# A recurrence of 64 blocks: which engine squares, sums and multiplies, and in which order the steps stand

## The chip, the cores and the metric

The kernel runs on one core of a Trainium2 chip. A core has five engines with instruction streams of their own: PE (TensorE, matrix products into PSUM), DVE (VectorE), ACT (ScalarE), POOL (GpSimd) and SP (SyncE, here only for starting transfers). They meet at semaphores. 16 DMA engines carry the transfers that SP and POOL start. The metric is the device time of one execution in microseconds; lower is better. Everything is float32.

## The reference, cut to what matters

The model has four layers on an image of 256 x 256 pixels with 128 channels, each of the form x + layer(group_norm(x)): an attention, a recurrence in the frequency domain, a triangle multiplication and a 3 x 3 convolution. The change lies in the second:

```python
forget_gate = sigmoid(x @ Wf + bf + 2.0)
input_gate  = sigmoid(x @ Wi + bi)
delta       = softplus(x @ Wd + bd) * 0.1
A_f, B_f    = fft2(padded A), fft2(padded B)      # complex, per channel
mag   = sqrt(Ar**2 + Ai**2 + 1e-08)
scale = 0.95 * sigmoid(mag) / (mag + 1e-08)
Ar, Ai = Ar * scale, Ai * scale
Bx_r, Bx_i = Br*x_r - Bi*x_i, Br*x_i + Bi*x_r
inp = delta * input_gate * Bx                     # both halves
# 16 times:
h_r, h_i = fg_r*(Ar*h_r - Ai*h_i) + inp_r, fg_i*(Ar*h_i + Ai*h_r) + inp_i
```

h starts at zero, and x + h goes to the third layer, whose group norm needs the mean and the mean square of x + h for every group of 4 channels.

## The kernel before

The 16 steps are not looped over. For each pixel and channel they are the power of a 2 x 2 matrix, and the kernel works out the power's coefficients from the trace t and the determinant d by repeated doubling (tr2, tr4, tr8 from tq2, tq4, tq8 and dn2, dn4, dn8), and then the sum of powers by one division, 1/(1 + d - t), made as an exponential of a logarithm.

The image is cut into NB = 64 blocks of 4 rows, 1024 pixels. The 128 channels are 64 real and 64 imaginary parts. In the recurrence's layout the 64 channels stand on half of the partitions, two of the block's rows on each half, so that a "wide" tile is 128 x 1024 (real and imaginary parts side by side) and a "thin" one is 128 x 512. A block goes through some 60 named steps. Those that the texts below speak of:

- ld: SP loads xf (channels by pixels, for the gates), xc (the same values in the layout of the recurrence) and hs (rows of the spectra of A and B).
- za, zb: the spectra of A and B in PSUM, from hs by PE. a2: the squares of A's parts (ACT; its tile is `a` in the profile). m2: their sum, |A|^2. lm, mg, lb, iv: the square root and the inverse of |A| by Ln and Exp on ACT; sg: the sigmoid; s: the scale. zaa: A copied to SBUF (`ar`).
- zd, zf, zi: the products of the gates; ab, ae, al_, q: softplus; f, ig: the sigmoids; fs_: f times s; ff: the product of f's halves, pf: their sum (POOL; tile `fs`). t (POOL) and d_ from these, D_ = d + 1 - t, lD and eD its inverse.
- p0, p1, bx: B times x. qg, v: the input term, in two halves.
- tq2 ... tq16, dn2 ... dn8 (squares on ACT), tr2 ... tr8, u2, u4, u8, xa, xb, be, e_, al: the doubling and the coefficients. xb is a sum on PE in PSUM (`pxb`).
- y0, y1, av, yf, yb and t1: A times v, times f, times its coefficient; and v times its own.
- ac1, ac2: the two terms are added to xc in SBUF by accumulating transfers that POOL starts. ev, bn: the sum and the sum of squares of the result, by ACT with an accumulator (tile `x2q`). st: the result goes to x2T in DRAM.

The steps are software-pipelined by hand. A list `order` holds pairs (step, lag); round `it` carries out each step for block it - lag, in the list's order, and `pin` holds each engine to that order. The loads are not pinned. So each engine's queue is fixed, and in it an instruction that waits holds up all behind it. The lags go to 4, so there are 68 rounds.

PSUM has three tags in this stage: "z" (two buffers of two banks, taken in turn by za, zb, zd, zf, zi), "y" (one buffer of two banks: av and bx) and "s" (two of one bank: m2 and pxb). `tt` and `stt` are two-input instructions on DVE (lines 995 and 1001 in the profile), `gt` one on POOL (998), `act` one on ACT (55), `mm` a matrix product (61). After the last round `warm` products keep PE running, the sums are reduced, and the triangle's stage begins with `tap_products` (products of the convolution's weights, for the fourth layer) and `group_affine` (the group norm's scale and shift from stats2).

Of the kernel before, what the change touches and what calls it, by code (L numbers as in the profile page):

```python
# [31 lines left out]
class Kernel:  # L32
# [50 lines left out]
    def group_affine(self, pool, psum, stats, tag, shift=None, mv=None, busy=8):  # L83
# [3 lines left out]
        pm = psum.tile([P, 2], F32, name=f"pm{tag}", tag="gn")  # L87
        d, v, mg, sd = (pool.tile([P, 1], F32, name=f"{n}{tag}") for n in ("gd", "gv", "mg", "sd"))
        if mv is None:
            mv = pool.tile([P, 2], F32, name=f"mv{tag}")  # L90
            V.tensor_reduce(mv, stats, AX.X, ALU.add)
            self.keep_busy(psum, busy)
            pin(self.mm(pm, self.g4n, mv))
            self.keep_busy(psum, 3)
            V.tensor_tensor(d, pm[:, 0:1], shift, ALU.add)
            V.scalar_tensor_tensor(v, d, d, pm[:, 1:2], ALU.mult, ALU.subtract)
            V.tensor_copy(mg, pm[:, 0:1])
            self.chain("table", self.act(sd, v, AF.Sqrt, bias=self.eps, scale=-1.0))
        else:
            self.keep_busy(psum, busy)  # L100
            pin(self.mm(pm[:, 0:1], self.g4, mv[:, 0:1]))
            self.keep_busy(psum, 3)
            V.tensor_copy(mg, pm[:, 0:1])
            V.tensor_sub(d, mv[:, 0:1], mg)
            V.scalar_tensor_tensor(v, d, d, mv[:, 1:2], ALU.mult, ALU.add)
            pv = psum.tile([P, 2], F32, name=f"pv{tag}", tag="gn")
            pin(self.mm(pv[:, 0:1], self.g4, v))
            self.keep_busy(psum, 3)
            self.chain("table", self.act(sd, pv[:, 0:1], AF.Sqrt, bias=self.eps))
# [797 lines left out]
    def recurrence(self, x1T, x2T, HD_, stats1, shift1, stats2, shift2):  # L907
# [7 lines left out]
        with ExitStack() as c:  # L915
# [39 lines left out]
            D = [{} for _ in range(NB)]  # L955
            parts = wp.tile([P, 2, 2, NB], F32, name="parts2")
            shiftc = wp.tile([P, 2], F32, name="shiftc")
            V.tensor_copy(shiftc, abc[:, :, 1])
            fold = wp.tile([P, HC], F32, name="fold")
            V.tensor_tensor(fold, self.ident[:, :HC], self.ident[:, HC:], ADD)  # L960
            rows = lambda t: t.rearrange("p i (r v) -> p r i v", v=N)
# [12 lines left out]
            def load(b):  # L974
                d = D[b]
                xf = d["xf"] = io.tile([P, 1024], F32, name="xf", bufs=2)
# [5 lines left out]
                d["hs"] = self.first_rows if b == 0 else self.row_transforms(io.tile([P, 2, HC], F32, name="hs", bufs=2), HD_, b)  # L982
# [34 lines left out]
            def total(d, name, pairs):  # L1017

                n = len(pairs)
                z = d[name] = ps.tile([P, n, 512], F32, name=name, tag="y" if n == 2 else "s", bufs=1 if n == 2 else 2)  # L1020
# [17 lines left out]
            def a2(d): act(rows(wide(d, "a2")), d["za"], AF.Square)  # L1038
            def m2(d): total(d, "m2", [[(self.ident, d["a2"][:, 0]), (self.ident, d["a2"][:, 1])]])
            def lm(d): act(thin(d, "mag"), d["m2"][:, 0], AF.Ln, bias=1e-8)  # L1040
# [5 lines left out]
            def ab(d): halves(d, wide(d, "az"), "d", "zd", AF.Identity)  # L1046
            def ae(d): act(wide(d, "ex"), d["az"], AF.Sigmoid, scale=-1.0)
            def al_(d): act(d["ex"], d["ex"], AF.Ln, bias=1e-37)
            def q(d): stt(wide(d, "q", 2), d["ex"], -1.0, d["az"], MUL, MAX)

            def sg(d): act(d["mag"], d["mag"], AF.Sigmoid)
            def s(d): tt(thin(d, "s", 3), d["mag"], d["inv"], MUL)
# [4 lines left out]
            def zaa(d): act(wide(d, "ar", 2), d["za"].rearrange("p r i v -> p i r v"), AF.Copy)  # L1057
# [3 lines left out]
            def t(d): gt(thin(d, "t", 3), d["fs"], d["ar"][:, 0], MUL)  # L1061
            def d_(d): tt(thin(d, "d"), d["m2"][:, 0], d["ff"], MUL)
            def D_(d): stt(thin(d, "D", 2), d["d"], 1.0, d["t"], ADD, SUB)

# [18 lines left out]
            def dn2(d): squared(d, "dn2", "d", 2)  # L1083
            def tr2(d): stt(thin(d, "tr2"), d["d"], -2.0, d["tq2"], MUL, ADD)
            def u2(d): gt(thin(d, "u2", 2), d["t"], d["tr2"], MUL)
            def tq4(d): squared(d, "tq4", "tr2")
# [3 lines left out]
            def tq8(d): squared(d, "tq8", "tr4")  # L1090
            def dn8(d): squared(d, "dn8", "dn4", 2)
# [3 lines left out]
            def xa(d): stt(thin(d, "g", 2), d["t"], -2.0, d["u8"], ADD, MUL)  # L1095
# [11 lines left out]
            def al(d): tt(d["t"], d["u8"], d["t"], SUB)  # L1107

            def y0(d): tt(wide(d, "y0"), d["ar"], both(d["v"][:, 0]), MUL)
            def y1(d): tt(wide(d, "y1"), d["ar"], both(d["v"][:, 1]), MUL)  # L1110
            def av(d): real_and_imaginary(d, "av", d["y0"], d["y1"])
            def yf(d): tt(wide(d, "yf", 2), d["av"], d["f"], MUL)
            def t1(d): (tt if last(d) else gt)(wide(d, "t1"), both(d["t"]), d["v"], MUL)
            def yb(d): tt(d["yf"], d["yf"], both(d["g"]), MUL)
# [13 lines left out]
            def ev_(d): statistic(d, 0, AF.Identity)  # L1128
            def bn(d): statistic(d, 1, AF.Square, shifted=True)
            def st(d):  # L1130
                b = d["b"]
                for half in range(2):
                    dst = x2T[:, b * 1024 + half * 512:b * 1024 + (half + 1) * 512]
                    pin(nc.gpsimd.dma_start(dst.rearrange("(r c) n -> c r n", c=HC), d["xc"][half * HC:(half + 1) * HC]))
            def ld(d): load(d["b"])
# [3 lines left out]
                (e_, 3), (ld, 0), (za, 0), (u4, 2), (zb, 1), (a2, 0), (av, 2), (t, 1), (p1, 1), (zaa, 0), (m2, 0),  # L1139
                (tq8, 2), (al, 3), (zd, 0), (ev_, 4), (lD, 2), (q, 1), (yf, 2), (p0, 1), (tq2, 1), (dn2, 1), (tr2, 1),  # L1140
                (eD, 2), (tr8, 2), (lm, 0), (dn8, 2), (mg, 0), (ab, 0), (t1, 3), (qg, 1), (lb, 0), (tq16, 2), (bx, 1),
                (ac1, 3), (iv, 0), (u8, 2), (yb, 3), (zf, 0), (sg, 0), (tq4, 1), (v, 1), (y1, 1), (f, 0), (xa, 2),
                (D_, 1), (s, 0), (u2, 1), (ac2, 3), (tr4, 1), (ae, 0), (fs_, 0), (zi, 0), (y0, 1), (ff, 0), (pf, 0),
                (xb, 2), (ig, 0), (be, 2), (al_, 0), (bn, 4), (d_, 0), (dn4, 1), (st, 4),
            )
            deep = max(lag for _, lag in order)
            for it in range(NB + deep):
                for step, lag in order:
# [3 lines left out]
            warm = ps.tile([P, 1, 512], F32, name="warm", tag="s")  # L1152
            for _ in range(56):
                pin(self.mm(warm[:, 0, :P], self.ident, self.cmat))
            red = wp.tile([P, 2, 2], F32, name="partsum")
            V.tensor_reduce(red, parts, AX.X, ADD)
            pr = ps.tile([P, 2], F32, name="partps", tag="s")
            for ri in range(2):
                self.mm(pr[ri * HC:(ri + 1) * HC], fold, red[:, :, ri])
            V.tensor_copy(stats2[:, :, 0], pr)  # L1160

    def triangle(self, x2T, x3T, znT, prodD, rs2D, rs3D, stats2, shift2, stats3, shift3, prepare):
# [12 lines left out]
        with ExitStack() as c:  # L1175
            wp = c.enter_context(self.pool(name="tw", bufs=1))
            with self.pool(name="twp", bufs=2, space=PSUM) as ps0:
                self.tap_products(ps0)
                ab, mg, _ = self.group_affine(wp, ps0, stats2, "2", shift=shift2, busy=0)
# [351 lines left out]
    def tap_products(self, ps):  # L1531

        W, V = self.weights, self.nc.vector
        kt, wd = W["kt"], W["wd"]
        pb = ps.tile([P, 2], F32, name="cpb", tag="gn")
        self.mm(pb[:, 0:1], wd, W["bv"])
        V.tensor_copy(W["bw"], pb[:, 0:1])
        for t in range(3):
            pk = ps.tile([P, 3, P], F32, name="cpk")
            for n in range(3):  # L1540
                self.mm(pk[:, n], kt[:, 3 * t + n, :], wd)
            V.tensor_copy(kt[:, 3 * t:3 * t + 3, :], pk)
# [178 lines left out]
    def run(self, ctx):  # L1721
# [10 lines left out]
        stats["2"] = const.tile([P, 2, 1], F32, name="stats2")  # L1732
        shift2 = const.tile([P, 1], F32, name="shift2")
# [87 lines left out]
```

## Time and profile before

| | |
|---|---|
| time, median of 3 runs | 4684.48 us (4682.95 to 4684.81) |
| profiled execution: its own time, its span | 4678.77 us, 4677.0 us |
| busy share of the span: PE, DVE, ACT, POOL | 97%, 80%, 71%, 45% |
| recurrence, first matmul of za to the first of the sums at the end | 1649.8 to 2973.6 us |
| DMA share and rate in the recurrence (1712 to 2894 us) | 0.57 of 16 engines, 131 GB/s |

The profile is of one execution, the trace behind it lists each instruction with its engine, start, duration and what released it. Three things help in reading it. A row of the groups gives busy time, mean duration and the idle time of the engine ahead of it; durations of neighbours on an engine overlap by some hundredths of a microsecond, so a sum of durations is a little over the time from start to start. An instruction that stands still after it has begun counts as busy: its duration grows, and no idle time shows. And the busy share of the whole span says little here, since the four layers have different limits; the windows give it by stage.

### The profile page before, as it was taken

What the parts mean: (1) busy time and instruction counts of PE and PEld (TensorE: products, weight loads), DVE (VectorE), ACT (ScalarE), POOL (GpSimd) and SP (SyncE); (2) the same over time, 40 slices, a digit from 0 to 9 for tenths busy, and PEclk for the clock granted to TensorE, in tenths of its full rate; (3) what the DMA queues carried; (4) which work ended last, traced back from release to release, by engine and by line L of the source; (5) the groups of instructions that cost most, each with busy time, mean ns of one, the idle gap of its engine ahead of it and who ended that gap; (6) DMA issues with size and microseconds to landing.
All of it is one profiled execution on the core that took longest, in us unless ns stands there. A gap on an engine that the chain in (4) does not pass through costs nothing. (4 is left out here: it accounts for less than half of the span.)

```text
span 4677.0 us, 79571 instructions
## 1 busy us (share of the span) xinstructions
PE 4521.0 (97%) x30445; PEld 2600.4 (56%) x30445; DVE 3750.3 (80%) x4827; ACT 3333.0 (71%) x5173; POOL 2101.5 (45%) x1379
## 2 busy tenths in 40 slices
PE   8999999999999989999999999899999999999999
PEld 2444555555555533333333333456999973379999
DVE  7776777777777679999999999787666677789885
ACT  7556888888888889999999999798443454442110
POOL 1333555555555547667666667333231245520000
PEclk9999999999999999999999999999999999999999
DMA  9892122222222235555555555576667758955432
GB/s 316 327 357 110 54 83 82 87 82 82 85 88 82 69 88 132 134 133 130 134 130 133 136 129 126 184 253 246 243 222 262 251 211 327 360 208 174 135 114 72
DMA packets 219655, 768.19 MB, mean 164 GB/s; under 512 B 58443, under 2 KB 60620, under 8 KB 178926
## 3 DMA queue, kind: packets, MB, share of 16 engines
q1 hardware_dynamic: 153976, 465.15, 29.2%
q0 software_dynamic: 65232, 297.90, 22.2%
q8 instruction: 244, 4.00, 0.3%
q14 instruction: 139, 1.14, 0.1%
q10 hardware_dynamic: 64, 0.00, 0.0%
HBM read 431.32 MB, written 265.55 MB: 149 GB/s over the span
## 5 line engine op out<-in xcount | busy, mean ns | idle before, releaser
L629 DVE TENSOR_TENSOR e<-sc,bT 128x1024 f32<-128x1024 f32 x512 | 613.8, 1220 | 255.8 <-PE sc L61 254.8
L629 POOL TENSOR_TENSOR ks<-e 128x1024 f32<-128x1024 f32 x256 | 602.4, 2371 | 443.2 <-PE nd L61 429.9
L55 ACT ACTIVATE e<-e 128x1024 f32<-128x1024 f32 x512 | 539.3, 1053 | 40.3 <-DVE e L629 30.7
L61 PE MATMUL m<-U,v 128*128 128x128 f32 x4608 | 514.8, 275 | 1.5 <-DVE v L1656 1.5
L61 PEld LDWEIGHTS m<-U,v 128*128 128x128 f32 x4608 | 514.6, 192 | 1.7 <-DVE v L1656 1.7
L61 PEld LDWEIGHTS z<-wf,zt 128*128 128x128 f32 x4096 | 462.6, 192 | 53.6 <-DVE LR L1169 28.0
L61 PE MATMUL z<-wf,zt 128*128 128x128 f32 x4096 | 474.8, 277 | 5.6 <-DVE LR L1169 5.5
L1169 DVE TENSOR_TENSOR LR<-z,sg 128x512 f32<-128x512 f32 (+1 forms) x323 | 270.0, 867 | 165.3 <-ACT sg L55 165.3
L1169 POOL TENSOR_TENSOR zt<-zt,df 128x512 f32<-128x512 f32 x127 | 161.5, 1271 | 423.2 <-ACT df L55 423.2
L55 ACT ACTIVATE sg<-z 128x512 f32<-128x512 f32 (+1 forms) x323 | 160.7, 509 | 243.7 <-PE z L61 241.4
L61 PE MATMUL sc<-proj 32*128 32x256 f32 x4096 | 300.5, 404 | 3.2 <-DVE e L629 2.4
L998 POOL TENSOR_TENSOR fs<-f 128x512 f32<-128x512 f32 x64 | 176.4, 2756 | 275.1 <-DVE f L995 251.1
L61 PEld LDWEIGHTS sc<-proj 32*128 32x128 f32 x4096 | 188.5, 185 | 161.8 <-PE px L61 94.8
L61 PE MATMUL nd<-e,proj 128*32 128x256 f32 x4096 | 273.7, 385 | 2.6 <-DVE og L629 2.6
L55 ACT ACTIVATE dn<-dn 128x512 f32<-128x512 f32 x384 | 237.9, 620 | 12.5 <-DVE dn L629 8.5
L1696 ACT COPY m4s<-m 128x512 f32<-128x512 f32 x32 | 18.7, 585 | 304.3 <-PE m L61 304.3
L61 PE MATMUL z<-LR 128*128 128x256 f32 x1024 | 225.5, 383 | 7.5 <-DVE LR L1169 7.5
L998 POOL TENSOR_TENSOR u<-t,tr 128x512 f32<-128x512 f32 x64 | 225.6, 3525 | 11.9 <-DVE tr L1001 10.1
L998 POOL TENSOR_TENSOR t<-t,v 128x1024 f32<-128x1024 f32 x63 | 206.9, 3285 | 50.2 <-DVE t L995 49.5
L1706 POOL DMA_DIRECT2D out_dram<-ys x32 | 37.0, 1157 | 420.9 <-DVE ys L1704 420.9
L61 PEld LDWEIGHTS z<-LR 128*128 128x128 f32 x1024 | 196.6, 192 | 35.5 <-DVE LR L1169 8.3
L1169 POOL TENSOR_TENSOR zt<-ga,zt 128x1024 f32<-128x1024 f32 x62 | 144.7, 2353 | 118.5 <-DVE ga L1169 118.5
(430 smaller groups left out, 10738.4 us busy)
## 6 DMA issues: line engine op xcount, KB each, us to landing
zt<-znT SPq DMA_DIRECT2D x96, 1024.0 KB
zt<-x2T SPq DMA_DIRECT2D x64, 1024.0 KB
xin<-in_x_dram SPq DMA_DIRECT2D x48, 1024.0 KB
xr<-x3T SPq DMA_DIRECT2D x46, 768.0 KB
x1T<-x POOLq DMA_DIRECT2D x64, 512.0 KB, 5.0
xf<-x1T SPq DMA_DIRECT2D x64, 512.0 KB
xc<-x1T SPq DMA_DIRECT2D x128, 256.0 KB
x2T<-xc POOLq DMA_DIRECT2D x128, 256.0 KB, 3.7
```

Source lines behind the costliest of these rows:

```text
L55: return self.nc.scalar.activation(out, in_, func, bias=bias, scale=scale, **kw)
L61: return self.nc.tensor.matmul(out, lhsT, rhs, start=start, stop=stop)
L629: pin = lambda f: lambda *a, **k: tc.keep_in_program_order(f(*a, **k))
L998: pin(nc.gpsimd.tensor_tensor(out, a, b_, op))
L1169: pin = lambda f: lambda *a, **k: tc.keep_in_program_order(f(*a, **k))
L1696: nc.scalar.copy(m4, m[4])
L1706: nc.gpsimd.dma_start(out[row:row + 8].rearrange("r p t c -> p (r t) c"), ys.rearrange("p g k t c -> p (g k t) c"))
```

## The change

What it does, by engine:

- |A|^2 (m2) is no longer two products on PE into PSUM: a2's first half gets its second added by an accumulating transfer that POOL starts (block 0: by DVE). lm and d_ read it from SBUF.
- The spectrum of A is made twice: za as before, and zc in the next round. ar holds only its real part, half the size, for t; y0 and y1 read zc in PSUM.
- The sum of the result (ev) is no longer taken by ACT: each block's xc is added to a tile `summed` by an accumulating transfer that POOL starts, reduced once at the end. The last block's sum is still ACT's.
- d_, al and yb go from DVE to POOL, u2 and t1 from POOL to DVE. st is started by SP, not by POOL.
- xf has one buffer, not two; hs four, not two; az, ex, a2, s, t, D, tq4, tq8 and others have other counts. Tag "s" in PSUM has one buffer; a bank is taken by `spare`, for `awake`.
- The order and the lags are new: the path to t and d is one round longer (lb, iv, sg, s, fs_, ff, pf, d_ at lag 1), the doubling of tr2 to u2 is at lag 2.
- tap_products comes ahead of the third round. The mean and mean square of the groups come from `folded` at the end of the recurrence, so that group_affine needs no reduction and no product for them.

```diff
-    def group_affine(self, pool, psum, stats, tag, shift=None, mv=None, busy=8):
+    def group_affine(self, pool, psum, stats, tag, shift=None, mv=None, busy=8, means=None):
...
+            if means is None:
+                ...
+            else:
+                pm = means
...
+            spare = ps.tile([P, 512], F32, name="spare", bufs=1)
+            def awake(n):
+                for _ in range(n):
+                    pin(self.mm(spare[:, :P], self.ident, self.cmat))
+            V.memset(parts, 0.0)
+            summed = io.tile([P, 2, 512], F32, name="summed", bufs=1)
+            nc.gpsimd.memset(summed, 0.0)
+            folded = wp.tile([P, HC], F32, name="folded")
+            V.tensor_tensor(folded, self.g4n[:, :HC], self.g4n[:, HC:], ADD)
...
-                xf = d["xf"] = io.tile([P, 1024], F32, name="xf", bufs=2)
+                xf = d["xf"] = io.tile([P, 1024], F32, name="xf", bufs=1)
...
-                ... self.row_transforms(io.tile([P, 2, HC], F32, name="hs", bufs=2), HD_, b)
+                ... self.row_transforms(io.tile([P, 2, HC], F32, name="hs", bufs=4), HD_, b)
...
-                z = d[name] = ps.tile([P, n, 512], F32, name=name, tag="y" if n == 2 else "s", bufs=1 if n == 2 else 2)
+                z = d[name] = ps.tile([P, n, 512], F32, name=name, tag="y" if n == 2 else "s", bufs=1)
...
-            def a2(d): act(rows(wide(d, "a2")), d["za"], AF.Square)
-            def m2(d): total(d, "m2", [[(self.ident, d["a2"][:, 0]), (self.ident, d["a2"][:, 1])]])
-            def lm(d): act(thin(d, "mag"), d["m2"][:, 0], AF.Ln, bias=1e-8)
+            def a2(d): act(rows(wide(d, "a2", 2)), d["za"], AF.Square)
+            def m2(d):
+                if d["b"]:
+                    pin(nc.gpsimd.dma_start(d["a2"][:, 0], d["a2"][:, 1], accum_op=ADD))
+                else:
+                    tt(d["a2"][:, 0], d["a2"][:, 0], d["a2"][:, 1], ADD)
+            def lm(d): act(thin(d, "mag"), d["a2"][:, 0], AF.Ln, bias=1e-8)
...
-            def zaa(d): act(wide(d, "ar", 2), d["za"].rearrange("p r i v -> p i r v"), AF.Copy)
+            def zaa(d): act(thin(d, "ar", 2).rearrange("p (r v) -> p r v", v=N), d["za"][:, :, 0], AF.Copy)
...
-            def d_(d): tt(thin(d, "d"), d["m2"][:, 0], d["ff"], MUL)
+            def d_(d): gt(thin(d, "d"), d["a2"][:, 0], d["ff"], MUL)
...
-            def u2(d): gt(thin(d, "u2", 2), d["t"], d["tr2"], MUL)
+            def u2(d): tt(thin(d, "u2", 2), d["t"], d["tr2"], MUL)
...
-            def al(d): tt(d["t"], d["u8"], d["t"], SUB)
-            def y0(d): tt(wide(d, "y0"), d["ar"], both(d["v"][:, 0]), MUL)
-            def y1(d): tt(wide(d, "y1"), d["ar"], both(d["v"][:, 1]), MUL)
+            def al(d): gt(d["t"], d["u8"], d["t"], SUB)
+            def zc(d): spectrum(d, 0, "zc")
+            def turned(d, n, k):
+                v = d["v"][:, k].rearrange("p (r v) -> p r v", v=N).unsqueeze(2).to_broadcast([P, 2, 2, N])
+                tt(rows(wide(d, n)), d["zc"], v, MUL)
+            def y0(d): turned(d, "y0", 0)
+            def y1(d): turned(d, "y1", 1)
...
-            def t1(d): (tt if last(d) else gt)(wide(d, "t1"), both(d["t"]), d["v"], MUL)
-            def yb(d): tt(d["yf"], d["yf"], both(d["g"]), MUL)
+            def t1(d): tt(wide(d, "t1"), both(d["t"]), d["v"], MUL)
+            def yb(d): gt(d["yf"], d["yf"], both(d["g"]), MUL)
...
-            def ev_(d): statistic(d, 0, AF.Identity)
+            def ev_(d):
+                if last(d):
+                    statistic(d, 0, AF.Identity)
+                else:
+                    pin(nc.gpsimd.dma_start(summed, d["xc"], accum_op=ADD))
...
-                    pin(nc.gpsimd.dma_start(dst..., d["xc"][half * HC:(half + 1) * HC]))
+                    pin(nc.sync.dma_start(dst..., d["xc"][half * HC:(half + 1) * HC]))
...
             order = (
-                (e_, 3), (ld, 0), (za, 0), (u4, 2), (zb, 1), (a2, 0), (av, 2), (t, 1), (p1, 1), (zaa, 0), (m2, 0),
-                (tq8, 2), (al, 3), (zd, 0), (ev_, 4), (lD, 2), (q, 1), (yf, 2), (p0, 1), (tq2, 1), (dn2, 1), (tr2, 1),
-                (eD, 2), (tr8, 2), (lm, 0), (dn8, 2), (mg, 0), (ab, 0), (t1, 3), (qg, 1), (lb, 0), (tq16, 2), (bx, 1),
-                (ac1, 3), (iv, 0), (u8, 2), (yb, 3), (zf, 0), (sg, 0), (tq4, 1), (v, 1), (y1, 1), (f, 0), (xa, 2),
-                (D_, 1), (s, 0), (u2, 1), (ac2, 3), (tr4, 1), (ae, 0), (fs_, 0), (zi, 0), (y0, 1), (ff, 0), (pf, 0),
-                (xb, 2), (ig, 0), (be, 2), (al_, 0), (bn, 4), (d_, 0), (dn4, 1), (st, 4),
+                (q, 1), (ld, 0), (zd, 0), (tq2, 2), (tr2, 2), (ab, 0), (tq4, 2), (za, 0), (dn2, 2), (D_, 2), (lD, 2),
+                (zb, 1), (a2, 0), (qg, 1), (lb, 1), (av, 2), (iv, 1), (ac2, 4), (tr4, 2), (tq8, 2), (e_, 3), (zaa, 0),
+                (u2, 2), (dn4, 2), (p0, 1), (dn8, 2), (p1, 1), (yb, 3), (zf, 0), (eD, 2), (yf, 2), (zi, 0), (tr8, 2),
+                (al, 3), (u4, 2), (m2, 0), (ev_, 4), (sg, 1), (st, 4), (ae, 0), (f, 0), (bx, 1), (t1, 3), (s, 1),
+                (ac1, 3), (ig, 0), (u8, 2), (fs_, 1), (tq16, 2), (xa, 2), (ff, 1), (pf, 1), (d_, 1), (t, 1), (al_, 0),
+                (zc, 1), (lm, 0), (xb, 2), (v, 1), (bn, 4), (y0, 1), (mg, 0), (y1, 1), (be, 2),
             )
             for it in range(NB + deep):
+                if it == 2:
+                    self.tap_products(ps)
...
-            warm = ps.tile([P, 1, 512], F32, name="warm", tag="s")
-            for _ in range(56):
-                pin(self.mm(warm[:, 0, :P], self.ident, self.cmat))
+            awake(56)
+            V.tensor_reduce(parts[:, 0, :, 0:1], summed, AX.X, ADD)
...
+            for n, m in enumerate((folded, fold)):
+                for ri in range(2):
+                    pin(self.mm(pr[ri * HC:(ri + 1) * HC, n], m, red[:, :, ri]))
+            awake(3)
...
-                self.tap_products(ps0)
-                ab, mg, _ = self.group_affine(wp, ps0, stats2, "2", shift=shift2, busy=0)
+                ab, mg, _ = self.group_affine(wp, ps0, stats2, "2", shift=shift2, means=self.means2)
```

In tap_products itself the products and copies are pinned, and its tiles take tag "s".

## The prediction

> **What bounds the kernel now.** I read the windows by stage first. The changed stage, the recurrence, runs from about 1650 to 2974 us. Its steady part was cut at the start of one DVE instruction (`q<-q,ig`, step qg) in two blocks 51 apart, 1832.29 and 2860.40:
>
> ```profile
> core 0: us, PE busy (x) PEld busy (x) DVE busy (x) ACT busy (x) POOL busy (x), PEclk, DMA share, GB/s
> 1712.00:2894.00 1182.00, 1121.29 (x3410) 393.36 (x3409) 1173.96 (x1470) 1173.95 (x1986) 808.96 (x469) 1.00 0.57 131
> 1832.29:2860.40 1028.11, 976.19 (x2959) 341.85 (x2958) 1020.40 (x1277) 1022.50 (x1735) 698.79 (x409) 1.00 0.57 132
> ```
>
> 1028.11/51 is a period of 20.16 us a block. ACT is busy 20.05 of it, DVE 20.01, PE 19.14, POOL 13.7; TensorE's granted clock is 1.00, so there is no throttle to win back. Two engines are full. Which one binds is told by the DVE's and POOL's timelines (start, duration), two excerpts of each:
>
> ```profile
> 1891.54 0.69 DVE L1001 SCALAR_TENSOR_TENSOR tr<-d,tq 128x512 f32<-128x512 f32 x1 [0.34 <-ACT tq L55]
> 1892.15 0.68 DVE L1001 SCALAR_TENSOR_TENSOR tr<-dn,tq 128x512 f32<-128x512 f32 x1
> 1892.75 2.30 DVE L995 TENSOR_TENSOR q<-q,ig 128x1024 f32<-128x1024 f32 x1
> ...
> 2215.88 1.22 DVE L995 TENSOR_TENSOR q<-q,ig 128x1024 f32<-128x1024 f32 x1
> ...
> 2218.75 1.21 DVE L1001 SCALAR_TENSOR_TENSOR v<-q,bx 128x1024 f32<-128x1024 f32 x1
> ```
>
> ```profile
> 1892.33 1.65 POOL L998 TENSOR_TENSOR u<-t,tr 128x512 f32<-128x512 f32 x1
> ...
> 2215.49 4.48 POOL L998 TENSOR_TENSOR u<-t,tr 128x512 f32<-128x512 f32 x1
> ```
>
> In two blocks of three POOL's u stands still under DVE instructions with two SBUF inputs (qg, u4, yb) and ends when v, with one input in PSUM, has run: 4.48 us for 1.3 us of work. In the third block DVE has caught up with ACT and waits 0.34 us for tq; POOL gets in, and qg stands still: 2.30 for 1.22. The 2.30 rows stand 60.47 us apart, three blocks. Between them DVE's block is 19.65 (tr4 at 1852.42 and 1872.08). So ACT binds at 20.05 to 20.16; DVE alone would need 19.65.
>
> The rows that the change touches (1700 to 2900, 60 blocks; busy, mean ns, idle), DVE, ACT, PE, POOL:
>
> ```profile
> L995 DVE TENSOR_TENSOR y<-ar,v 128x1024 f32<-128x1024 f32 x119 | 145.4, 1221 | 2.0
> L995 DVE TENSOR_TENSOR u<-u,tr 128x512 f32<-128x512 f32 x119 | 81.3, 683 | 0.0
> L995 DVE TENSOR_TENSOR yf<-yf,g 128x1024 f32<-128x1024 f32 x59 | 71.7, 1216 | 0.0
> L995 DVE TENSOR_TENSOR d<-m,ff 128x512 f32<-128x512 f32 x60 | 40.8, 680 | 0.0
> ```
>
> ```profile
> L55 ACT ACTIVATE x2q<-xc 128x512 f32<-128x512 f32 x118 | 74.0, 627 | 1.9
> L55 ACT ACTIVATE ar<-za 128x1024 f32<-128x1024 f32 x60 | 60.8, 1013 | 0.0
> ```
>
> ```profile
> L61 PE MATMUL m<-a,ident 128*128 128x512 f32 x240 | 118.6, 617 | 24.1 <-ACT a L55 24.1
> L61 PE MATMUL za<-ev,hs 14*128 14x512 f32 x240 | 67.6, 640 | 0.0
> ```
>
> ```profile
> L998 POOL TENSOR_TENSOR t<-t,v 128x1024 f32<-128x1024 f32 x60 | 198.0, 3300 | 42.4 <-DVE t L995 41.7 <-DMA hs<-HD 0.7
> L998 POOL TENSOR_TENSOR fs<-f 128x512 f32<-128x512 f32 x60 | 167.0, 2783 | 233.9 <-DVE f L995 233.9
> ```
>
> **The change, per block.** *ACT.* ev goes (two x2q with their accumulator reads: 2211.55 to 2212.92, 1.37), ar is halved (0.91 from start to start becomes about 0.48, a 512 row's), lm reads SBUF (+0.04): 20.05 - 1.37 - 0.43 + 0.04 = 18.3. Table loads stay two a block, since Ln/Exp and Sigmoid steps are still in two groups.
>
> *DVE.* From start to start a 512 instruction costs 0.60, a 1024 one 1.14 (2215.88 to 2217.01). Off: d_ and al (0.60 each) and yb (1.14). On: u2 (0.60), t1 (1.14). That is -0.60. y0 and y1 now read zc in PSUM in a strided order; nearest are yf<-av,f (PSUM, plain, 1217 ns, as dear as SBUF) and p (PSUM, strided, 740 against 684 for 512): between 0 and +0.11 each; I take +0.06 each. 19.65 - 0.60 + 0.12 = 19.17.
>
> *PE.* m2 goes (118.6/60 = 1.98), zc comes (za's row, 1.13): 19.14 becomes 18.3. In the new order zb waits for ab to free zd's buffer, about 0.45. By distances of starts (zf 1.77, bx 3.6, pxb 2.6, za 0.95) the round is 18.0, with that wait 18.4.
>
> *POOL.* u2 and t1 leave; d_, al and yb come; st's two issues (1.30) move to SP, and m2 and ev are two issues more (0.9 each, by xc<-t's 0.94). Unblocked work: 512 1.30 (t<-fs,ar), 1024 2.36 (t<-t,v in the tail). When can it run? The Trainium skill (SBUF — State Buffer, Who interferes with whom) has VectorE with two SBUF inputs and GpSimd reading SBUF exclude each other for a whole instruction. The excerpts agree, which speaks against more POOL work: 5 x 1.3-2.4 = 7.6 us has to lie where DVE reads PSUM or rests. By the rule alone those 7.6 us and DVE's 11.2 us of two-SBUF work (four of 1.14, eleven of 0.60) fill 18.8 of a round of 19.17, and nothing is lost; by the trace an instruction that enters at the wrong time costs the other engine 1.08 (2.30 - 1.22), five of them 5.4. Which it is, the order decides. So I lay DVE out by starts: q 0, tr2 1.13, D_ 1.73, qg 2.33, tr4 3.46, e_ 4.06, u2 4.66 (all SBUF); p0 5.26, p1 6.57, yf 7.88 (PSUM); tr8 9.02, u4, t1 10.22, s, u8, fs_ 12.56, xa 13.70, ff 14.30 (SBUF); v 14.90, y0, y1, be (PSUM), end about 19.17. yb and al need 3.66 in the first gap of 3.76; pf, d_ and t, whose input ff ends at 14.98, need 3.9 in the second of 4.2. Both fit, barely. I add 0.1 for overlaps at their ends: **19.27 a block**.
>
> *What the new waits hold up.* t (POOL) ends about 18.9 and releases tq2, then tr2, due at 1.13 of the next round: about 0.5 spare. Behind it ACT has ab, tq4, dn2 for tr4 at 3.46, 0.4 spare, if zd ends by 0.7. u2 on DVE needs only t and tr2, which are there. POOL's queue: ac2 waits for ac1's landing (issued 11.5, 4.9 to land, needed at 19), ev for ac2's (landed about 6, needed 10), then ac1; ev may be 3 us late before pf is. m2 is issued at about 9 and lm, its reader, comes at 16.4, against 4.9 for twice the bytes. DMA: queue 0 took 38.4% of 1200 us, 7.7 a block for 1.5 MB; 0.75 MB more, 3.9, brings the share from 11.5 of 20.16 to some 15.4 of 19.27. SP: xf 0.34, xc 1.35, eight hs 7, st 1.30, 10 of 19; st waits for ac2, with the next loads behind it, at a time when these need xf's buffer anyway. xf has one buffer now: its load starts after zi (about 10.5) and zd wants it at 18.
>
> *Ends.* tap_products moves from PE's path before pm (2973.9 to 2978.4) into the third round: three turns of 1.45 matmul, 0.56 copy and handovers, 6.6, partly beside a pipe still filling (DVE busy 41.3 of the first 62): +4. In the triangle's start gd comes 4.8 earlier (2979.03 against about 2974.2), but the loads of zt still go out at 2974: -3.5. ev of the block before the last leaves ACT's tail: -1.5. For the last block yb and al on POOL in line (3.66) replace 2.6 on the DVE: +1. Sum 0; from -6 to +7.
>
> **Sum.** 64 x (20.16 - 19.27) = 57. The profiled execution (span 4677.0, 4678.8 in all) would become 4621.8; the median of the runs lies 5.7 above it, so 4684.5 - 57 = **4627.5**.
>
> **Rivals.** *Single xf buffer (PE late).* Two transfers of 512 KB took 2201.5 to 2206.2 together, 0.21 MB/us. Beside m2, ev and ac1 xf gets half: 4.7 us plus issue and landing, at 16 to 17, 1 to 2 before zd's need. If it takes over 7.5 us, zd, ab, dn2 and tr4 slip. Half a microsecond late: 19.75, 4684.5 - 26 = 4658. For: SP's queue is in order, with hs between. Against: the room.
> *POOL takes the port (slower).* yb is queued from about 0.8 while DVE runs q to u2. If DVE pauses there (tq2 over 0.5 late, or dn2), yb starts and holds the port 2.36; the next DVE instruction waits about 2.15 (1.08 per 1.30 in the trace, less the overlap). In every block: 21.4, +80, 4764. It eats the gain from 0.89/2.15 = 41% of the blocks. For: the trace shows just this for u, one block in three. Against: there ACT was the late one; it has 0.9 spare now, and fs, queued behind f in the same way, lost 60 of 60 times (2778 to 2796 ns).
> *The transfers do not do what they should.* An accumulation within SBUF of 256 KB is not in the trace. From 3.0 to 7.2 us (the extremes of xc's transfers, issue to landing) it is hidden; at 9.2 us lm waits 1.9, ACT is at 20.2 again, and the time stays 4684. For: two transfers more on one queue. Against: its half size, and that nothing else of that queue is under way at 9.
>
> **How the numbers follow.** Laid out as above 0.62 (19.1 to 19.55: 4610 to 4650); xf late 0.16 (faster); port taken 0.16, of which slower 0.12 and within the bound 0.04; transfers 0.06, of which faster 0.01, same 0.03, slower 0.02. Faster by over 0.2% (9 us, what a measurement here can tell): 0.79; same 0.07; slower 0.14. The range 4606 to 4684 leaves out the slower cases and the edges.
>
> **What would show it.** Right: 19.2 to 19.4 a block; DVE 99%, ACT about 95%; rows x2q<-xc only at the end; yb starting as p0 does, about 2.4 long after its wait; ff at 684 ns. Wrong: DVE rows of 2.3 to 3.5 us among D_, qg and ff; lm waiting for a DMA; zd waiting for xf; PE's clock below 1.00 in the middle.

## The result, and the profile after

The change makes the kernel slower: 4782.5 us (median of 4 runs, 4779.5 to 4786.8) against 4684.65 for the kernel before (4 runs, 4682.95 to 4684.9). The ratio is 1.0214, 95% interval 1.0202 to 1.0226. The forecast was 4627.5. What came is the rival "POOL takes the port", in every block, and a second loss that had no price in the forecast: TensorE's clock.

The windows of the changed kernel, from one start of qg to the start 50 blocks later (the columns are those of the windows of before):

```profile
1796.84:2877.58 1080.74, 1012.66 (x2900) 344.34 (x2899) 1061.44 (x1202) 938.43 (x1501) 639.04 (x450) 0.93 0.75 160
```

1080.74/50 is 21.615 us a block; before it was 20.16. DVE is busy 98% of it, ACT 87%, PE 94%, and TensorE's granted clock has fallen from 1.00 to 0.93. So ACT was relieved as planned, and DVE has become the full engine, at a block 2.3 us longer than the 19.27 worked out for it. Where those are is read from DVE's timeline, with POOL's beside it:

```profile
2202.50 1.22 DVE L1015 SCALAR_TENSOR_TENSOR q<-ex,az 128x1024 f32<-128x1024 f32 x1
2203.64 2.83 DVE L1015 SCALAR_TENSOR_TENSOR tr<-d,tq 128x512 f32<-128x512 f32 x1
...
2218.98 0.68 DVE L1009 TENSOR_TENSOR ff<-f 128x512 f32<-128x512 f32 x1
2220.34 1.22 DVE L1015 SCALAR_TENSOR_TENSOR v<-q,bx 128x1024 f32<-128x1024 f32 x1 [0.68 <-PE bx L61]
2221.66 2.35 DVE L1009 TENSOR_TENSOR y<-zc,v 128x1024 f32<-128x1024 f32 x2
2224.17 0.69 DVE L1015 SCALAR_TENSOR_TENSOR g<-pxb,D 128x512 f32<-128x512 f32 x1 [0.15 <-PE pxb L61]
```

```profile
2202.67 3.25 POOL L1012 TENSOR_TENSOR yf<-yf,g 128x1024 f32<-128x1024 f32 x1
```

yb is issued 0.17 us after q has begun, stands until q is through, and then runs for its 2.36 us. tr2, which reads two tiles in SBUF, stands for that time: 2.83 us for 0.68. (This exclusion of DVE and POOL is what the texts call the port.) As with qg before, the time shows as a long instruction and not as idle time. It is so in every block, as the groups tell (busy and mean duration, then the idle time ahead):

```profile
L1015 DVE SCALAR_TENSOR_TENSOR tr<-d,tq 128x512 f32<-128x512 f32 x51 | 145.0, 2843 | 0.0
L1009 DVE TENSOR_TENSOR y<-zc,v 128x1024 f32<-128x1024 f32 x102 | 120.1, 1219 | 5.3
L1009 DVE TENSOR_TENSOR ff<-f 128x512 f32<-128x512 f32 x51 | 34.5, 676 | 0.0
```

```profile
L55 ACT ACTIVATE tq<-tr 128x512 f32<-128x512 f32 x167 | 104.9, 628 | 103.2 <-DVE tr L1015 103.2
```

```profile
L61 PE MATMUL zf<-xf,gwf 128*64 128x512 f32 x440 | 131.1, 726 | 55.7 <-ACT ar L55 55.7
L61 PE MATMUL zd<-xf,gwd 128*64 128x512 f32 x448 | 108.5, 605 | 0.9 <-DMA xf<-x1T 0.9
```

tr2's mean of 2843 ns stands against 686 in the kernel before: 2.15 us a block. ff is at its 676, so the second gap of POOL's work came out as laid out. ACT's squares wait 103 us for tr2, and PE then waits for ACT ahead of zf, 1.0 us a block in the mean. Two blocks in three take 21.26, and 21.26 - 2.15 = 19.11 is close to the layout of the forecast (19.17). The third takes 22.27, since there v waits for bx. bx is late because PE ran at half speed for a while. The clock in a slow stretch and behind it:

```profile
2211.67:2215.08 3.41, 3.41 (x10) 0.98 (x8) 3.41 (x6) 3.36 (x6) 1.16 (x2) 0.50 1.06 218
2215.10:2220.00 4.90, 4.90 (x16) 1.73 (x12) 4.56 (x6) 4.87 (x8) 2.24 (x2) 1.00 0.83 192
```

The granted clock is either 1.00 or 0.50, and a slow stretch lasts 3.41 us or a multiple. In the steady part (1792 to 2860) of the changed kernel there are 41 of them, in that of the kernel before none.

### The profile page after: what moved, and what is told of

Same layout as the page of the kernel before. It is cut to its first block, busy times and chain, and to the rows that moved or that the text cites. A ratio compares the mean times of both kernels' runs of the same rounds, so it can differ in the third digit from the quotient of the medians.

```text
span 4777.7 us, 79502 instructions
## 1 busy us (share of the span) xinstructions
PE 4597.8 (96%) x30447; PEld 2611.1 (55%) x30447; DVE 3827.2 (80%) x4766; ACT 3251.6 (68%) x4922; POOL 2040.1 (43%) x1443
## 3 DMA queue, kind: packets, MB, share of 16 engines
q14 instruction: 138, 1.13, 0.1%
## 5 line engine op out<-in xcount | busy, mean ns | idle before, releaser
L632 DVE TENSOR_TENSOR e<-sc,bT 128x1024 f32<-128x1024 f32 x512 | 613.1, 1219 | 255.8 <-PE sc L61 254.8
L61 PE MATMUL av<-y,ident 128*128 128x512 f32 x384 | 222.1, 691 | 0.0
L61 PE MATMUL zf<-xf,gwf 128*64 128x512 f32 x512 | 152.6, 726 | 61.8 <-ACT ar L55 61.5
L1012 POOL TENSOR_TENSOR yf<-yf,g 128x1024 f32<-128x1024 f32 x64 | 204.9, 3202 | 10.4 <-DVE g L1015 10.4
L55 ACT ACTIVATE tq<-tr 128x512 f32<-128x512 f32 x192 | 120.6, 628 | 119.3 <-DVE tr L1015 119.3
```

Of the source, the lines that this page charges most:

```text
L55: return self.nc.scalar.activation(out, in_, func, bias=bias, scale=scale, **kw)
L61: return self.nc.tensor.matmul(out, lhsT, rhs, start=start, stop=stop)
L632: pin = lambda f: lambda *a, **k: tc.keep_in_program_order(f(*a, **k))
L1012: pin(nc.gpsimd.tensor_tensor(out, a, b_, op))
```

## Experiments

Each starts from the changed kernel. Only the lines that differ are shown. Times are medians; the kernel before, timed beside each batch, had 4682.1, 4687.8, 4680.7 and 4681.1 us. "A block" is the mean distance of q's starts in the steady part.

### The port: is it yb, and what lets it in?

**e1, m2's start ahead of yb.** POOL's queue is in order, and m2 waits for ACT's a2. So yb can't be issued before about the end of u2.

```diff
-                (u2, 2), (dn4, 2), (p0, 1), (dn8, 2), (p1, 1), (yb, 3), ... (u4, 2), (m2, 0), (ev_, 4), ...
+                (u2, 2), (dn4, 2), (p0, 1), (dn8, 2), (p1, 1), (m2, 0), (yb, 3), ... (u4, 2), (ev_, 4), ...
```

> Edit: in the order of the changed kernel (m2, 0) stands right ahead of (yb, 3), so that POOL's yb is queued behind the issue of m2, which waits for a2 on ACT (about 4.7 us into the round); nothing else moves on DVE, ACT or PE. Theory port: in the changed kernel yb is queued 0.17 us after q has begun on DVE, takes the port that POOL and DVE share when q ends, and tr2 stands still 2.15 us in every block. With yb queued at about 5.4 us it meets p0 and p1, which read PSUM: tr2 at about 0.68 us instead of 2.83, the period from 21.6 to between 19.2 and 20.3 (the upper end if yb and al run into tr8 and t1), the time between 4629 and 4700. Rival clock: the rests of PE ahead of zf, and the halved clock after them, set the period; they do not depend on yb's place: 4770 or more. Rival transfers: the new accumulating transfers make their readers late: no change, about 4782.

Measured: 4720.1 us, ratio to before 1.0075 (1.0058 to 1.0091); 20.47 us a block.

```profile
L1015 DVE SCALAR_TENSOR_TENSOR tr<-d,tq 128x512 f32<-128x512 f32 x44 | 30.1, 685 | 0.0
```

tr2 is back at 685 ns, and the kernel 62 us faster than the change. So the entry of yb was the largest term. But 20.47 is above the range given, and not 19.27: POOL, now later, holds ff in 17 of 54 blocks (mean 1048 ns) and stands in the way of the tr4/tr8 group (mean 816), zd begins to wait for xf, and the clock is 0.95.

**e2, yb on DVE.**

```diff
-            def yb(d): gt(d["yf"], d["yf"], both(d["g"]), MUL)
+            def yb(d): tt(d["yf"], d["yf"], both(d["g"]), MUL)
```

> Edit: in the changed kernel yb alone goes back from POOL to DVE, at its place in the order. DVE has 1.14 us more work a block. Theory port: the 2.15 us in tr2 go, 21.6 becomes 19.1 + 1.14 = 20.25 a block, 4697 us. Rivals clock and transfers: DVE's extra work comes on top or beside, 4782 or up to 70 more.

Measured: 4714.2, ratio 1.0064 (1.0047 to 1.0081); 20.47 a block, 20.25 in the shortest, as 19.11 + 1.14 has it; the longer ones bring the time to 17 us over the forecast, and the clock's slow stretches are all still there (42). tr2 684 ns. The port's loss goes with yb, by another way.

**e3, ev on ACT again.** It takes one of the four accumulating transfers away and gives ACT its 1.37 us back.

```diff
-                if last(d):
-                    statistic(d, 0, AF.Identity)
-                else:
-                    pin(nc.gpsimd.dma_start(summed, d["xc"], accum_op=ADD))
+                statistic(d, 0, AF.Identity)
```

> Edit: in the changed kernel the sum of the result (ev) is taken by ACT again, as before; the accumulating transfer into summed goes, 512 KB a block. Theory port: DVE's stand in tr2 stays; ACT gets 1.4 us more of which it has about 2 idle: from 4775 to 4815. Rival transfers: the transfer into summed is what delays the others, DMA share 0.74 falls, and the time falls by 20 us or more.

Measured: 4843.2, ratio 1.0342 (1.0325 to 1.0359), above every range given; 22.61 a block, DMA share 0.57. The transfer was not the trouble: without it the kernel is 60 us slower. yb still got in (tr2 2834 ns), and now pf did too, under ff:

```profile
L1009 DVE TENSOR_TENSOR ff<-f 128x512 f32<-128x512 f32 x40 | 70.4, 1760 | 0.0
```

**e4, qg and e_ between q and tr2.** If POOL's instruction simply follows the one that runs when it is issued, another victim takes tr2's place.

```diff
-                (q, 1), (ld, 0), (zd, 0), (tq2, 2), (tr2, 2), ... (a2, 0), (qg, 1), (lb, 1), ... (tq8, 2), (e_, 3), (zaa, 0),
+                (q, 1), (ld, 0), (zd, 0), (tq2, 2), (qg, 1), (e_, 3), (tr2, 2), ... (a2, 0), (lb, 1), ... (tq8, 2), (zaa, 0),
```

> Edit: in the changed kernel qg and e_ go ahead of tr2 on DVE, so that q is followed by qg (a plain two-input instruction, TENSOR_TENSOR), e_ (SCALAR_TENSOR_TENSOR, nothing of another engine to wait for) and tr2 (SCALAR_TENSOR_TENSOR, waits for ACT's tq2). All have two SBUF inputs. yb is queued on POOL 0.17 us after q has begun, as before. Theory port: time within 40 us of 4782, with one DVE row of about 2.15 us over its own duration. Which row tells what lets POOL in: reading first come: qg stands, 3.3 us; reading form (POOL gets in ahead of a SCALAR_TENSOR_TENSOR, a TENSOR_TENSOR keeps the port): qg 1.2, e_ 2.8; reading semaphore (POOL gets in ahead of an instruction that waits for another engine): qg 1.2, e_ 0.7, tr2 2.8. Rivals clock and transfers: no row has to stand.

Measured: 4959.4 (one run), 24.44 a block.

```profile
L1009 DVE TENSOR_TENSOR q<-q,ig 128x1024 f32<-128x1024 f32 x37 | 120.2, 3249 | 1.3
L1015 DVE SCALAR_TENSOR_TENSOR tr<-d,tq 128x512 f32<-128x512 f32 x37 | 25.1, 678 | 0.0
```

It is neither tr2's form nor its wait for tq2: whatever stands next after q is held, here qg, 3.25 us for 1.21, as the first of the three readings had it. The time lies far outside its 40 us: with the moved steps al and pf get in as well (D_ 1757, ff 1761 ns).

Why did yb get in behind q, when POOL's fs in the kernel before, issued during y0, stayed out behind y0 and ff too, until be read PSUM? In the changed kernel DVE rests just before: 0.10 us at y0, which reads v's result straight after v (2221.66 above), or 0.15 at be.

**e7, v ahead of ff**, so that y0 does not follow v. **e8** is the same with two buffers for xf (the edit is shown at e9).

```diff
-                (xa, 2), (ff, 1), (pf, 1), (d_, 1), (t, 1), (al_, 0), (zc, 1), (lm, 0), (xb, 2), (v, 1), (bn, 4), (y0, 1), ...
+                (xa, 2), (v, 1), (ff, 1), (pf, 1), (d_, 1), (t, 1), (al_, 0), (zc, 1), (lm, 0), (xb, 2), (bn, 4), (y0, 1), ...
```

> The changed kernel with one step moved in the order: v stands ahead of ff (fs_, xa, v, ff, y0, y1, be), so that y0 no longer follows the instruction whose result it reads. Theory 'recent rest': POOL's queued yb gets the port at the end of q because DVE had rested (0.10 us at y0, or 0.15 at be) within the three instructions before. Then, if be doesn't wait for pxb either, yb stands until p0, tr2 is 0.69 us, the period falls from 21.6 to 19.3-19.9 and the time to 4640-4680. If be still waits for pxb in a part of the blocks, yb wins in just those. Theory 'whoever is queued when q runs gets it': nothing changes, tr2 2.8 us, 21.3-21.7 us a block, 4770-4790.

> The same with two buffers for xf again. If the block is now short enough for the single buffer to bind (zd waiting for xf's transfer), this is faster than with v ahead of ff alone, by what zd waited there (up to 0.3-0.5 us a block, 20-30 us). If not, the two agree within 5 us. 'Whoever is queued gets it': 4770-4790 as without.

Measured: e7 4726.1, ratio 1.0091 (1.0072 to 1.0109), 20.68 a block; e8 4712.9, ratio 1.0063 (1.0045 to 1.0081), 20.38. One moved step is worth 56 us, so "whoever is queued gets it" is wrong. But both lie above the 4640 to 4680 of the rest theory: blocks of 18.92, in which yb stays out, alternate with blocks of 21.08, in which it gets in, and most of those follow a rest at v, which waited for a slowed bx.

**e13 and e16** were to take that rest away: e13 is e8 with a filler on PE (see e11) that mends the clock. e16 also moves ACT's mg behind tq2, so that tr2's input is there earlier.

```diff
-                (q, 1), (ld, 0), (zd, 0), (tq2, 2), (tr2, 2), ... (y0, 1), (mg, 0), (y1, 1), (be, 2),
+                (q, 1), (ld, 0), (zd, 0), (tq2, 2), (mg, 1), (tr2, 2), ... (y0, 1), (y1, 1), (be, 2),
```

> The changed kernel with v ahead of ff, two xf buffers and the filler of 128 rows, m2 left behind yb (without the filler: 20.38 us a block, 4712.9; yb took the port in 17 of 54 blocks, each time five instructions after v had waited for a slowed bx). 'Recent rest' theory with a steady TensorE: v no longer waits, yb stands until p0 in nearly every block, tr2 0.7 us, 18.95-19.4 us a block, 4610-4645. If yb gets the port for another reason: 20.2-21.3, 4700-4770.

> The kernel with v ahead of ff, two xf buffers and the filler of two products (20.34 us a block, 4709.8; yb not held by m2), and ACT's mg moved from ahead of tq2 to behind it, so that tq2 ends 0.1-0.2 us earlier. 'tr2's input has to be there early': tq2 now ends at 0.5 or before in each block, yb stays out, tr2 0.7 us, 19.0-19.4 us a block, 4625-4655. 'It is not tq2': yb gets in as often as before, 20.1-20.5, 4700-4715.

Measured: e13 4709.8, ratio 1.0061 (1.0044 to 1.0078), 20.34 a block; e16 4713.7, ratio 1.0071 (1.0055 to 1.0088), 20.49. Both miss the range that the rest theory gave. In e16 tq2 ended 0.46 to 0.49 us after q's start, and yb got in as often as before (in 27 of 53 blocks, in e13 in 25 of 54): it is not tq2. Two neighbouring blocks of e16, POOL's yb, and then DVE's xa (tile `g`), v, q and tr2:

```profile
2156.91 7.24 POOL L1012 TENSOR_TENSOR yf<-yf,g 128x1024 f32<-128x1024 f32 x1
2176.97 2.64 POOL L1012 TENSOR_TENSOR yf<-yf,g 128x1024 f32<-128x1024 f32 x1
```

```profile
2151.37 0.67 DVE L1015 SCALAR_TENSOR_TENSOR g<-t,u 128x512 f32<-128x512 f32 x1
2151.97 1.20 DVE L1015 SCALAR_TENSOR_TENSOR v<-q,bx 128x1024 f32<-128x1024 f32 x1
...
2156.57 1.20 DVE L1015 SCALAR_TENSOR_TENSOR q<-ex,az 128x1024 f32<-128x1024 f32 x1
2157.70 0.67 DVE L1015 SCALAR_TENSOR_TENSOR tr<-d,tq 128x512 f32<-128x512 f32 x1
...
2170.29 0.67 DVE L1015 SCALAR_TENSOR_TENSOR g<-t,u 128x512 f32<-128x512 f32 x1
2170.92 1.22 DVE L1015 SCALAR_TENSOR_TENSOR v<-q,bx 128x1024 f32<-128x1024 f32 x1
...
2175.53 1.21 DVE L1015 SCALAR_TENSOR_TENSOR q<-ex,az 128x1024 f32<-128x1024 f32 x1
2176.66 3.51 DVE L1015 SCALAR_TENSOR_TENSOR tr<-d,tq 128x512 f32<-128x512 f32 x1
```

In the first block yb is issued 0.34 us into q and stands 4.9 us, behind six DVE instructions after q, until p0 reads PSUM. That makes POOL late, so that in the next block yb comes 1.44 after q's start, 0.31 into tr2, and runs almost at once: 2.64 us in all, and tr2 ends 0.55 after it. Counted over the seven kernels in which yb is free to come at q (the change, e3, e7, e8, e13, e14, e16; 363 blocks):

| | yb gets in | yb stays out |
|---|---|---|
| DVE was idle (over 0.02 us) ahead of q or of one of the five instructions before it | 209 | 0 |
| no such idle time, yb issued in the first 1.0 us of q | 2 | 85 |
| no such idle time, yb issued 1.0 to 3.0 us after q's start | 36 | 31 |

The 36 of the last row had a rest too, one too short to show as idle time, since neighbours overlap. The starts show it. v normally begins 0.60 us after xa (2151.97 after 2151.37). In these 36 blocks it begins 0.63 to 0.69 after it (2170.92 after 2170.29: bx's last product had ended at 2170.88), in the 31 at most 0.004 later than usual. Counted by late starts (0.03 us or more, of q or of one of the five before it), yb got in in 245 of 245 blocks that had one and in 2 of 118 that had none. The two, in e7, are unexplained.

So the filler in e13 and e16 did not take the rest away, it shortened it. When yb stays out, DVE's block is 18.92, while PE's round with the filler is 19.3; DVE gets ahead, v is early for bx, and the late start lets yb in a block later.

This is a count over blocks as they came. No run varies that wait alone, and the count is for yb at q. In e1 pf got in under ff in 17 of 53 blocks without a late start of ff or of the five before it, and stayed out in 36; what decides there is open.

### The clock

In the changed kernel's trace each of the 41 slow stretches follows a stretch of 3.41 us in which PE did za, rested, and did zb (25 of them), or rested for 2.1 us ahead of zf (16). One of the 25:

```profile
2225.93 1.13 PE L61 MATMUL za<-ev,hs 14*128 14x512 f32 x4
2227.36 1.20 PE L61 MATMUL zb<-ev,hs 14*128 14x512 f32 x4 [0.31 <-ACT az L55]
2228.49 1.87 PE L61 MATMUL av<-y,ident 128*128 128x512 f32 x2
```

The slow stretch begins at 2228.7: av's first pair takes 1.87 where it takes 1.13 at full clock. za and zb use 14 of the array's 128 rows ("14*128"); with the rest they are 2.64 us. In the kernel before they stand together without a rest.

**e9 and e10** clear the port first: e9 is e1 with two xf buffers, e10 has v ahead of ff too.

```diff
-                xf = d["xf"] = io.tile([P, 1024], F32, name="xf", bufs=1)
+                xf = d["xf"] = io.tile([P, 1024], F32, name="xf", bufs=2)
```

> The start of m2 moved ahead of yb, and two buffers for xf. With m2 ahead alone a block took 20.47 us. If zd's waits for xf made the difference to 19.4 (the shortest blocks), 19.6-19.9 us a block and 4650-4685. If POOL's remaining entries into the port did (al under tr8, pf under ff in 17 of 54 blocks), 20.2-20.5 and 4705-4720.

> All three: the start of m2 ahead of yb, two buffers for xf, v ahead of ff. 'Recent rest' theory: pf now runs beside v, so ff is no longer held (17 of 54 blocks times 1.07 us with m2 ahead alone), and yb is kept back by m2's wait whatever DVE does: 19.3-19.8 us a block, 4635-4665. If what cost the time with m2 ahead was neither ff nor zd but al under tr8: 20.0-20.5, 4690-4720.

Measured: e9 4700.1, ratio 1.0030 (1.0017 to 1.0043), 20.16 a block; e10 4690.7, ratio 1.0005 (0.9996 to 1.0014), 20.09. e9 lies between its two forecasts. e10 lies at the lower edge of its upper one, whose reason was to be al under tr8; but al holds tr8 in 23 blocks here, and in 51 of the faster e11 below. In e10 tr2, qg and ff all have their unblocked length, and DVE yet waits 0.44 us a block for av and 0.40 for bx. In its blocks without a slow stretch PE goes round in 19.11 us with a single rest of 0.31, ahead of zb; with a slow stretch the round is 20.80, 1.7 us more. PE is the bound, and its clock the loss:

```profile
1800.00:2700.00 900.00, 885.87 (x2606) 304.18 (x2604) 864.36 (x1079) 846.07 (x1350) 498.04 (x405) 0.95 0.81 172
```

**e11** fills the rest of e10 with two products of 128 rows into the bank `spare`. **e12** has the same with 14 rows (second diff), **e15** one product of 128 rows, awake(1).

```diff
+            def fill(d): awake(2)
...
-                ... (D_, 2), (lD, 2), (zb, 1), ...
+                ... (D_, 2), (lD, 2), (fill, 0), (zb, 1), ...
```

```diff
-            def fill(d): awake(2)
+            def fill(d):
+                for _ in range(2):
+                    pin(self.mm(spare[:, :P], self.ident[:14], self.cmat[:14]))
```

> The kernel with m2's start ahead of yb, two xf buffers and v ahead of ff (20.09 us a block, clock 0.95, 4690.7), and between za and zb two filler products of 128 rows (0.45 us) on PE. Theory 'idle rows': in the traces the half clock of 3.41 us follows a window of 3.41 us in which the array rows in use, weighted by time, were below about 0.38; za, a rest of 0.31 and zb use 14 of 128 rows at most for 2.6 us. The filler lifts such a window above 0.45: clock 1.00 in the steady part, PE's round 19.11 + 0.14, 19.3-19.6 us a block (al or another instruction of POOL under tr8 and tr4 in some blocks), 4635-4660. If the clock is not what holds this version: 20.0-20.2, 4685-4700.

> As the kernel with the filler, but the two filler products use 14 rows of the array, not 128 (same length, same place: TensorE has no rest either). 'Idle rows': the half clock stays, mean clock 0.94-0.96, 20.0-20.3 us a block, 4685-4705. 'The rest of 0.31 us as such is what halves the clock': 1.00 and 19.3-19.6, 4635-4660, as with full rows.

> The kernel with m2's start ahead of yb, two xf buffers, v ahead of ff, and one filler product of 128 rows between za and zb, not two (19.42 us a block and 4652.8 with two; there PE never rests and its round is 19.29). If PE's round is the bound: the filler of 0.23 us fits into the rest of 0.31, PE's round is 19.1, and a block takes 19.1-19.3, 4640-4650. If the window's use of rows counts: 0.38 + 0.07 is still above 0.38, clock 0.99-1.00. If one product is too little: clock 0.96, 19.9-20.1, 4680-4692.

| | us | ratio to before (95%) | a block | slow stretches in the steady part | PE's rests there |
|---|---|---|---|---|---|
| e10 | 4690.7 | 1.0005 (0.9996 to 1.0014) | 20.09 | 31 | 60, 17.0 us in all |
| e11, two full | 4652.8 | 0.9944 (0.9927 to 0.9961) | 19.42 | 4 | 0 |
| e12, two of 14 rows | 4677.25 | 0.9988 (0.9981 to 0.9995) | 19.84 | 22 | 12, 1.0 us in all |
| e15, one full | 4672.25 | 0.9985 (0.9976 to 0.9993) | 19.73 | 18 | 15, 1.1 us in all |

e11 met its forecast, and the windows show PE without a rest at a clock of 0.99, e12 just as full at 0.97:

```profile
1800.00:2700.00 900.00, 900.00 (x2867) 321.27 (x2867) 893.80 (x1111) 870.12 (x1390) 513.32 (x417) 0.99 0.82 178
```

```profile
1800.00:2700.00 900.00, 899.64 (x2824) 330.84 (x2820) 876.01 (x1092) 856.50 (x1364) 502.91 (x411) 0.97 0.80 174
```

e12 lies between its two forecasts. With next to no rest left, 22 slow stretches remain, and PE was busy all through the stretch ahead of each, so a rest is not needed for them. With full rows in the same place they nearly go. So the rows in use count, and the traces fit a rest that adds to the same account. e15 missed: one product fills most of the rest and is too little. A rough measure of the use is PE's busy time with each product over 14 rows weighted by 14/128 and all others by 1. Of the stretches of 3.41 us at full clock, in all traces here, none used for less than 0.34 of its length stayed without a slow one behind it, and none above 0.45 had one; in between both occur. In the kernel before the lowest is 0.46. That edge is read from the traces, not from a run that varies it finely, and the measure isn't exact: without the filler most slow stretches follow a use of 0.32 to 0.39, with it one of 0.44 to 0.45.

**e14, the filler in the changed kernel alone**, to size the clock's part there:

> The changed kernel with the filler of 128 rows between za and zb alone. The half clock after za, rest, zb goes (some 28 of 43 low windows of the steady part), those after the 2.1 us rest ahead of zf stay; yb still takes the port in every block (y0 still follows v at once): tr2 2.8 us, 21.2-21.5 us a block, 4755-4780. If the clock were the larger part of the loss: below 20.5, under 4715.

Measured: 4767.3, ratio 1.0182 (1.0165 to 1.0199), 21.29 a block, clock 0.98, tr2 2842 ns. The clock was 0.33 us a block of the change's loss, 15 us in all; the long third block is gone and the port's 2.15 stays. More slow stretches went than expected: 9 are left, of which one follows the rest ahead of zf.

### The single xf buffer

**e17** is e11 with one buffer for xf, as in the change.

> The kernel with m2's start ahead of yb, v ahead of ff and the filler of two products, with one buffer for xf as in the change (two: 19.42 us a block, 4652.8). The prediction's rival 'single xf buffer': zd waits for xf's transfer by up to 0.5 us in a part of the blocks, 19.6-20.0, 4665-4685. If the transfer has room: the same as with two within 6 us.

Measured: 4696.6, ratio 1.0032 (1.0018 to 1.0047), 20.36 a block: above its range.

```profile
L61 PE MATMUL zd<-xf,gwd 128*64 128x512 f32 x352 | 86.9, 613 | 30.8 <-DMA xf<-x1T 30.8
```

zd waits 0.7 us a block. The buffer costs 44 us once port and clock are out of the way; in the changed kernel zd waited for xf 0.9 us in all. A block of 21.6 gives the transfer more time; the change with two buffers and nothing else was not run.

## Why the prediction was wrong

- **What bounds the kernel before**: nothing contradicts it. With ACT at 18.8 (not the 18.3 of the sum) a block of 19.42 was reached in e11, below the 20.05 that ACT needed before.
- **DVE's sum, 19.17**: held, and was a little high. It is 19.11, or 18.92 with v ahead of ff, which is where the forecast's own starts end when they are carried on from v at 14.90 (three of 1.14, one of 0.60). Nearly all of the 0.19 between them is y0, which begins 0.17 late behind v. y0 and y1 from PSUM cost 1219 ns, as from SBUF: the 0.06 each were not needed.
- **The step that failed is the port: "yb and al need 3.66 in the first gap", with 0.1 us a block for overlaps.** It took for granted that yb, queued behind q, would stand until p0. In the changed kernel yb came 0.17 us after q's start and got in behind q in 51 of 51 blocks, which cost DVE 2.15 us a block. The rival named a condition, a pause of DVE "there", between q and u2. The pause that counts lies ahead of that, at y0 or be, in an order that puts y0 straight after v: 0.10 us of idle time, in a place not looked at. The evidence against the rival was weaker than it looked. fs, which "lost 60 of 60 times", lost to y0 and ff alone, and DVE's last rest, y1 0.11 us late straight after v, lay six instructions back. And u, in the same kernel, got in in just those 18 of 54 blocks in which tr2 had begun 0.1 us or more late, for tq2. The rival's price was right: about 2.15 for the next instruction, measured 2.15; 21.4 a block, measured 21.26 without the clock's part. It was given a chance of 0.16.
- **The rule of the Trainium skill** (SBUF — State Buffer, Who interferes with whom) held as to who excludes whom. That section also says: "Issue order, not op shape, decides who blocks." Here yb issued 0.34 us into q stayed out for six later DVE instructions in some blocks of e7 and got in behind q in others, so the order of issue alone does not decide; the measurement does.
- **TensorE's clock**: no term. "No throttle to win back" was read from the kernel before, and "PE's clock below 1.00 in the middle" stood as a sign without a price. It is 0.33 us a block in the changed kernel, 0.67 in e10. The Trainium skill (TensorE: Matmul & The Clock Gate, HAM oscillation — how this bites in real kernels) gives the rule "no PE-idle gaps >~3.4µs"; by it the changed kernel, with no rest of PE over 2.2 us in its steady part, would have kept its clock and taken some 21.3 a block (as e14 nearly does). The slow stretches do last 3.41 us, but a rest of 0.31 between products of 14 rows was enough, and in e12 almost none.
- **PE's round, 18.0 to 18.4**: too low. At full clock it is 19.11 with its rest of 0.31 (e10). With DVE at 19.27 this moved nothing in the forecast; it is the bound of e11 (19.29 with the filler), where PE is busy all of the 900 us.
- **Transfers**: held. m2 landed in 3.5 us, lm never waited, and with ev back on ACT (e3) the kernel is 60 us slower.
- **Single xf buffer**: not the loss in the changed kernel, but a real cost, 0.94 us a block in e17 against the 0.5 that the rival allowed.
- **The ends, 0**: +8. The products of the partial sums start 101.3 us later (3074.9 against 2973.6), 64 x 1.455 = 93 of it in the blocks, which leaves 8 for filling and emptying the pipe. Where these lie was not traced further.
- **The sum**: 19.27 predicted. 19.11 + 2.15 (yb at tr2) + 0.33 (clock) = 21.59 against 21.615 measured. 93 + 8 = 101; the medians differ by 98.

The best version is e11: the change with m2's start ahead of yb, two xf buffers, v ahead of ff and a filler of two products. It is 0.56% faster than the kernel before (0.39 to 0.73) and 130 us faster than the change as made. It misses the forecast's 19.27 a block by 0.15 and its time by 25 us; 10 of these are the blocks, and the rest lies outside the steady part. From the last start of q to the partial sums it takes 50.4 us against 36.8 before, but q also stands first in the new order and further down in the old one, so not all of these 14 are lost. Whether the longer path to t is the reason was not tried. In the steady part of e11 POOL's al still holds tr8 in 51 of 55 blocks, by 0.4 us, so DVE is 99% busy there too.

## What to carry to other kernels

Before work is moved from VectorE to GpSimd, find for each moved instruction where VectorE last rested ahead of the place where it will be queued. A wait of some hundredths of a microsecond, for a product of TensorE or for the result of the instruction just ahead, can let it in and cost VectorE nearly the whole length of GpSimd's instruction. Such waits show in the distance from start to start, not in the idle time. Hold it back by something ahead of it in GpSimd's queue rather than by hope. When matrix products that use few rows come together, look at the granted clock of the stage, and put a full product between them.

## What was not expected of the hardware

- An instruction of GpSimd that has been issued can stand up to 4.9 us behind six VectorE instructions that it excludes, or get in behind the first. For yb at q a late start of VectorE, of as little as 0.03 us, in q or the five instructions before went with it in 361 of 363 blocks; for pf at ff in e1 it did not.
- An instruction of VectorE that has begun (tr2, 0.31 us earlier by the trace) can still be held by one of GpSimd issued after it: 3.51 us for 0.67.
- TensorE was granted half its clock for 3.41 us after a stretch in which it was busy 91% of the time, and in e12 all of the time, much of it with products of 14 rows.
- Accumulating transfers within SBUF of 256 KB landed in 3.5 us, of 512 KB in 5.5 to 6.3, with four of them a block.
